# Patch layer of a four-layer network: one scan and one product with C per slot, on 1024 columns instead of 512

## The chip, the cores and the metric

The kernel runs on one core of a Trainium2 chip. The metric is the device time of one launch in microseconds. The kernel's four layers run one after the other in that launch; the change touches only the third, the patch layer (layer 2 in the code).

## The reference

Eight images of 96 channels and 64 x 64 pixels pass through four layers, each a residual: x = x + layer(group_norm(x)). Layer 2, cut to what matters here:

```
xin, z = split(in_proj(x));  z = silu(z)
t = gelu(batch_norm(conv3x3(xin)));  offset = tanh(conv1x1(t)) / 63
x_s = bilinear samples of xin at (pixel grid + offset)
patches: 16 positions each (4 x 4), every patch is a sequence of its own
for 4 directions k (rows, columns, and both reversed):
    delta = softplus(...);  B, C = 16 states each, from x_s
    h[l] = exp(delta[l] * A) * h[l-1] + delta[l] * u[l] * B[l]
    y[l] = sum over states of h[l] * C[l]  + D * u[l]
y = sum of the 4 directions, put back in order
out = out_proj(layer_norm(y) * z)
```

There are 192 inner channels, 16 states and 4 directions. A sequence has only 16 steps: the state starts anew in every patch.

## The kernel before

**Tiling.** An image is cut into 8 chunks of 512 positions, so there are 64 chunks. Within a chunk the recurrence runs over 4 directions x 6 blocks of 32 channels x 2 parts of the states, which makes 48 groups. A group's tile has 128 partitions (32 channels x 4 states) and two halves of 512 columns (two further sets of 4 states). The 32 patches of a chunk lie behind one another along the columns. At each patch's edge the step delta is overwritten with 1e25 (`FAR`, L1493), so the decay there is exp(-huge) = 0 and one long scan restarts at every patch.

**Slots.** The order of the work is written out by hand: `Slots.run` calls `slot(t)` for t in sequence, one slot per group, and what each engine issues in a slot is issued in that order. A chunk takes 48 slots (`PER`) beginning at slot B, and group t is the one scanned in slot t. In slot t:

- SP starts the load of the step sizes `dd` (delta and delta times u, repeated over states by the transfer) for the group six slots ahead (`AHEAD2`). Two groups share one load of 512 KB; four buffers rotate.
- ACT computes the decays `ps_d` of group t+1, exp(A * delta), one instruction per half (L336), into PSUM.
- ACT does the "first" side tasks of the slot: mostly copies of PE's results out of PSUM.
- DVE runs the scan of group t, one instruction per half (L1531), over the decays and in their place in PSUM.
- PE adds the product of group t-1 over the states into `ps_y` with a 0/1 matrix (`total`, L372), and then does its "pe" side tasks.
- ACT does its "act" side tasks.
- POOL computes `dbu` of group t+2, delta u times B, on both halves at once (L354). Then it does its "pool" side tasks.
- DVE multiplies the scanned halves of group t with C into `dbu`, one instruction per half (L364).

Three groups of a chunk's 48 are *late* (groups 2, 26 and 34 of the chunk): their scan writes into `dbu`, and the product with C is done on POOL a slot later (L359) instead of on DVE.

**Side tasks** carry the rest of the layer for this chunk and for the next two: the convolution for the offsets (L1227, copied by L1241, then gelu), the offsets (L1268, copied by L1279, then tanh), the sampling (POOL), the gate (L1396, copied by L1407, then silu), the softplus for delta (L1430 to L1493), the rows of B and C, the layer norm (L1596 to L1625) and the output (L1642 to L1666). Gelu, tanh and silu need another table in ACT than exp and ln, and each is framed by two table loads, the second one bringing back the table for exp.

**The rows of B and C.** `spread` loads, for each direction, 1024 KB of B (`brep`) and 1024 KB of C (`crep`) into SBUF, repeated over the channels. Two buffers of each rotate. The loads are issued by SP at slots T-11 and T-8, T being the direction's first slot; the directions of a chunk run one after the other, 12 slots each.

**Halves of the channels.** Groups of the first 96 channels add into `ps_y0`, those of the last 96 into `ps_y1`. After the first two directions, `rows` copies the sum out in the other pixel order (L1572); after the last two, `columns` adds that copy back with an identity matrix (L1578) and copies the final sum (L1584). `wds` times x (L1542) opens each bank with the D term.

**PSUM.** Eight banks of 512 float32 columns per partition. Decays: `ps_d0` and `ps_d1`, two buffers of one bank each. `ps_y0`, `ps_y1`: one bank each. `ps_k`: one bank for the convolution, the layer norm and the output. `ps_a`: one bank for everything else.

Of the kernel before, what the change touches and what calls it, by code (L numbers as in the profile page):

```python
# [21 lines left out]
NW = 512  # L22
# [224 lines left out]
AHEAD2, SPREAD2 = 6, 4  # L247

# [33 lines left out]
class Slots(Plan):  # L282
# [97 lines left out]
    def steps(self, T, out, f, pre, u, reset):  # L380
# [56 lines left out]
        for n, run in enumerate((add, lost, delta, delta_u)):  # L437
            self.at(T - 15 + 2 * n, "pool", run)

# [696 lines left out]
def layer2(S, src, dst, st_in, st_out, images, cp, W, ready, finish):  # L1136
# [3 lines left out]
    with ExitStack() as ctx:  # L1140
        psd = ctx.enter_context(tc.tile_pool(name="l2q", bufs=2, space=PSUM))
        psy = ctx.enter_context(tc.tile_pool(name="l2y", bufs=1, space=PSUM))
        psk = ctx.enter_context(tc.tile_pool(name="l2k", bufs=1, space=PSUM))
# [11 lines left out]
        sl = Slots(S, cp, wp, psd, "k_red2", GC2, AHEAD2, SPREAD2)  # L1155
# [35 lines left out]
        def front(ch, b, pad, xs, c, B):  # L1191
# [29 lines left out]
            def conv(m, k0, k1):  # L1221
                def run():
                    if k0 == 0:
                        ch["pk"] = new(psk, [128, NW], "ps_k")
                    for k in range(k0, k1):
                        dy, dx = k // 3, k % 3
                        nc.tensor.matmul(  # L1227
                            ch["pk"][:HD, :],
                            woff[:, k, m * HD : (m + 1) * HD],
                            pad[:, dy : dy + 8, dx : dx + IW],  # L1230
                            start=k == 0,
                            stop=k == KT - 1,
                        )

                return run
# [12 lines left out]
            for m, slots, last in (  # L1248
                (0, ((-86, 2), (-85, 2), (-84, 2), (-81, 2), (-80, 1)), -79),
                (1, ((-79, 2), (-67, 2), (-66, 1), (-62, 2), (-61, 2)), -60),  # L1250
            ):
                k = 0
                for t, taps in slots:
                    sl.at(B + t, "pe", conv(m, k, k + taps))
                    k += taps
                sl.at(B + last, "first", conv_out(m))
# [249 lines left out]
        def direction(ch, pr, xs, k, n, T):  # L1506
# [4 lines left out]
            def spread(name, what, t):  # L1511
                def run():
                    dr[name] = new(fp, [128, 4, NW], f"{name}rep", bufs=2)
                    at = n * 2 * NS + what * NS
                    nc.sync.dma_start(
                        dr[name].rearrange("p q l -> p (q l)"),
                        ch["rows"][at : at + NS]
                        .rearrange("(s q) l -> s (q l)", q=4)
                        .unsqueeze(0)
                        .to_broadcast([GC2, HS2, 4 * NW]),  # L1520
                    )

                sl.at(t, "sp", run)

            spread("b", 0, T - 11)
            spread("c", 1, T - 8)

            def scan(i, out, da, dbu):

                way = slice(None, None, -1 if k // 2 else 1)  # L1530
                nc.vector.tensor_tensor_scan(  # L1531
                    out[:, way], da[:, way], dbu[:, way], 0.0, ALU.mult, ALU.add
                )
# [3 lines left out]
            def y_of(h, g, part):  # L1537
                def run():
                    if g == 0 and part == 0 and n % 2 == 0:
                        ch["y", h] = new(psy, [128, NW], f"ps_y{h}")  # L1540
                        if n == 0:
# [4 lines left out]
                    first = n == 2 and g == 0 and part == 0  # L1546
                    return ch["y", h][:HD, :], first, n == 1 and g == HD // GC2 - 1 and part == 1
# [8 lines left out]
            for i in range(12):  # L1556
                part, g, h = i % 2, i // 2 % 3, i // 6
                at = 4 * (i // 2) + 2 * part
                sl.groups[T + i] = Group(
                    n=g, a=acol[:, k, at : at + 2], steps=steps_of(h, g), part=part,  # L1560
                    b=lambda p=part: dr["b"][:, 2 * p : 2 * p + 2, :],
                    c=lambda p=part: dr["c"][:, 2 * p : 2 * p + 2, :],
                    y=y_of(h, g, part), scan=scan, late=12 * n + i in (2, 26, 34),
                )

        def end(ch, im, b, c, B):
# [9 lines left out]
            def columns(h):  # L1576
# [12 lines left out]
                sl.at(B + 42 + 6 * h, "pe", pe)  # L1589
                sl.at(B + 43 + 6 * h, "first", act)  # L1590

            def centred(m):
                def pe():
                    ch["pk"] = new(psk, [128, NW], "ps_k")
# [13 lines left out]
                sl.at(B + 50 + m, "pe", pe)  # L1608
                sl.at(B + 51 + m, "first", act)

            def variance():
                ch["pk"] = new(psk, [128, NW], "ps_k")
# [24 lines left out]
            def out(n):  # L1637
                if n == 0:
                    ch["pk"] = new(psk, [128, NW], "ps_k")
# [30 lines left out]
            sl.at(B + 19, "first", rows(0))  # L1670
            sl.at(B + 25, "first", rows(1))
# [5 lines left out]
            for t, engine, run in (  # L1677
                (53, "pe", variance), (54, "first", root), (55, "dve", scaled),
# [4 lines left out]
            if c == NC - 1:  # L1683
                GroupStats(S, sl, B + 90, st_out[:, b, :], lambda: im["bns"], fp, psk, "ps_k")
# [5 lines left out]
        def piece(n, b, q, m, T0, T):  # L1690
            p, at = {}, slice(q * 1024, q * 1024 + 1024)

            def load():
                p["y"] = new(wp, [128, 1024], "dbu", bufs=6)
                if m < SPREAD2:
                    p["x"] = new(wp, [128, 1024], "dd", bufs=SPREAD2)
                else:
                    x = new(fp, [128, 4, NW], "brep", bufs=2)
# [25 lines left out]
        for n, b in enumerate(images[ready:]):  # L1724
            GroupStats(
                S, sl, 48 * n - 6, st_in[:, b, :], lambda n=n: late_bns[n], fp, psk, "ps_k", nm[b]
            )

        for n, b in enumerate(images):
            im = {"bns": new(fp, [CH, NC, 6], f"bns{n % 2}")}  # L1730
            for c in range(NC):
# [3 lines left out]
                for m, k in enumerate(ORDER):  # L1735
                    T = B + 12 * m
# [449 lines left out]
```

## Time and profile before

| what | value |
|---|---|
| median of 11 runs | 18204.22 us (18178.81 to 18226.62) |
| profiled execution, its own time | 18196.81 us |
| span of its profile | 18195.0 us |
| DVE busy over the span | 16311.3 us (90%) |
| POOL busy | 15215.9 us (84%) |
| PE busy | 13536.2 us (74%) |
| ACT busy | 9807.4 us (54%) |
| mean granted TensorE clock | 0.900 |
| first and last start of the patch layer's scans (L1531) | 3873.7 and 14360.8 us |

The profile is one execution. A row of a group gives line, engine, operation, output and inputs, count, busy time in us and mean ns of one, then the idle time ahead of it and what ended that. The mean of one instruction includes its tail, which overlaps with the next instruction on the same engine; the distance from start to start is shorter. A timeline row gives start, length, engine, line, operation and count; several equal instructions in a row are merged.

### The profile page before, as it was taken

The numbers are of one execution on the slowest core, as the hardware profiler recorded it, in microseconds if no ns is written. First come the engines' busy times: TensorE is split into PE (matmuls) and PEld (weight loads), VectorE is DVE, ScalarE is ACT, GpSimd is POOL, SyncE is SP. The second block draws the span as 40 slices with busy tenths as digits, with TensorE's granted clock in tenths as the row PEclk, the third lists the DMA queues.
The fourth block names the chain that finished last, engine by engine and source line by source line (L and its number), as shares of the span: only waits on it lengthen the run. The fifth ranks groups of instructions, "written<-read, shape, count | busy, mean of one in ns | idle before, by whom it ended". The sixth has DMA issues, their size and how long they took to land. (4 is left out here: it accounts for less than half of the span.)

```text
span 18195.0 us, 132874 instructions
## 1 busy us (share of the span) xinstructions
PE 13536.2 (74%) x32964; PEld 4957.7 (27%) x32964; DVE 16311.3 (90%) x16871; ACT 9807.4 (54%) x16056; POOL 15215.9 (84%) x9068
## 2 busy tenths in 40 slices
PE   8999998968888888888888888888888644434333
PEld 2323223722222222222222222222222211111111
DVE  7999998679999999999999999999999766767667
ACT  6777775556666666666666666666666311111100
POOL 7999996059999999999999999999999656565555
PEclk8999998979999999999999999999999866666666
DMA  7888886366666666666666666666666445444443
GB/s 127 148 150 150 149 149 116 64 157 135 132 134 133 134 134 134 134 134 135 134 134 134 134 134 133 134 135 134 134 133 133 114 134 153 140 143 136 136 128 121
DMA packets 802763, 2437.68 MB, mean 134 GB/s; under 512 B 259122, under 2 KB 260863, under 8 KB 734829
## 3 DMA queue, kind: packets, MB, share of 16 engines
q1 hardware_dynamic: 654541, 1976.06, 54.8%
q0 software_dynamic: 147456, 453.13, 8.2%
q8 instruction: 270, 4.42, 0.1%
q14 instruction: 496, 4.06, 0.1%
HBM read 1116.39 MB, written 104.46 MB: 67 GB/s over the span
## 5 line engine op out<-in xcount | busy, mean ns | idle before, releaser
L354 POOL TENSOR_TENSOR dbu<-dd,brep 128x1024 f32<-128x1024 f32 x3840 | 9020.0, 2364 | 136.0 <-DMA dd<-delta 108.2
L372 PE MATMUL ps_y<-dbu,k_red 128*96 128x512 f32 x15360 | 7506.4, 617 | 1581.4 <-DVE dbu L364 1250.7
L1531 DVE TENSOR_TENSOR_SCAN ps_d<-ps_d,dbu 128x512 f32<-128x512 f32 x5760 | 6713.0, 1209 | 79.6 <-POOL dbu L354 79.4
L336 ACT ACTIVATE ps_d<-dd,l_alog 128x512 f32<-128x512 f32 x7680 | 4989.2, 681 | 3321.9 <-DVE dbu L364 3109.9
L364 DVE TENSOR_TENSOR dbu<-ps_d,crep 128x512 f32<-128x512 f32 x7104 | 4490.9, 672 | 0.0
L372 PEld LDWEIGHTS ps_y<-dbu,k_red 128*96 128x96 f32 x15360 | 2384.6, 167 | 6346.1 <-issue 3707.4
L2020 POOL DMA_INDIRECT v<-t,idx x2304 | 2185.1, 948 | 1573.4 <-DVE s L2047 751.4
L2047 DVE TENSOR_REDUCE s<-v 128x864 f32<-128x3456 f32 x256 | 1554.7, 6073 | 373.7 <-remote 270.9
L2038 DVE TENSOR_TENSOR v<-v,ps_w 128x3456 f32<-128x3456 f32 x256 | 958.3, 3744 | 752.4 <-ACT ps_w L2030 699.6
L681 DVE TENSOR_TENSOR_SCAN ps_d<-ps_d,carry,dbu 128x512 f32<-128x512 f32 x1184 | 1452.9, 1272 | 94.3 <-POOL dbu L354 64.9
L2066 ACT COPY smp<-ps_t 128x768 f32<-128x768 f32 (+1 forms) x512 | 244.3, 529 | 1727.4 <-remote 997.0
L1227 PE MATMUL ps_k<-pad,woff 96*96 96x512 f32 x2304 | 1093.9, 597 | 26.5 <-ACT pad L1204 24.0
L2058 PE MATMUL ps_t<-k_ident,s 128*128 128x128 f32 (+1 forms) x1792 | 323.7, 332 | 955.0 <-issue 683.2
L359 POOL TENSOR_TENSOR dbu<-dbu,crep 128x1024 f32<-128x1024 f32 x288 | 677.8, 2354 | 293.8 <-issue 237.6
L1872 PE MATMUL ps_u<-k_ident,oc 27*128 27x27 f32 x256 | 33.0, 252 | 802.5 <-ACT oc L1867 719.0
L1855 PE MATMUL ps_a<-xpad,l_om 96*27 96x512 f32 x1152 | 592.5, 665 | 20.7 <-issue 20.5
L1227 PEld LDWEIGHTS ps_k<-pad,woff 96*96 96x96 f32 x2304 | 372.3, 164 | 667.5 <-issue 570.2
L2058 PEld LDWEIGHTS ps_t<-k_ident,s 128*128 128x128 f32 (+1 forms) x1792 | 249.6, 169 | 1083.8 <-issue 975.0
L2089 PE MATMUL ps_o<-smp,l_w 128*96 128x512 f32 (+1 forms) x896 | 466.6, 679 | 84.2 <-ACT smp L2066 61.4
L1469 POOL TENSOR_TENSOR sp_m<-sp_m,sp_s 128x512 f32<-128x512 f32 x384 | 489.6, 1275 | 32.2 <-ACT sp_s L1457 32.2
L1176 POOL MEMSET pad<- 96x660 f32 x4 | 2.4, 648 | 610.1 <-DMA y<-yb 610.1
L583 PE MATMUL ps_k<-xn,wk 96*96 96x512 f32 x1024 | 500.6, 612 | 3.1 <-ACT xn L557 2.4
(268 smaller groups left out, 15661.5 us busy)
## 6 DMA issues: line engine op xcount, KB each, us to landing
dd<-delta SPq DMA_DIRECT2D x2304, 512.0 KB
brep<-bcd SPq DMA_DIRECT2D x256, 1024.0 KB
crep<-bcd SPq DMA_DIRECT2D x256, 1024.0 KB
v<-t,idx POOLq DMA_INDIRECT x2304
xo<-x SPq DMA_DIRECT2D x128, 192.0 KB
x<-xo SPq DMA_DIRECT2D x128, 192.0 KB
bcd<-bc SPq DMA_DIRECT2D x64, 256.0 KB
xn<-x SPq DMA_DIRECT2D x64, 192.0 KB
```

What stands on the lines that cost most here:

```text
L336: nc.scalar.activation(da, g.dd[:, 0, :], AF.Exp, scale=g.a[:, i : i + 1])
L354: nc.gpsimd.tensor_tensor(g.dbu, g.dd[:, 1:2, :].to_broadcast([128, 2, NW]), g.b(), ALU.mult)
L359: nc.gpsimd.tensor_tensor(g.dbu, g.dbu, g.c(), ALU.mult)
L364: nc.vector.tensor_tensor(g.dbu[:, i, :], g.h[i], g.c()[:, i, :], ALU.mult)
L372: self.S.nc.tensor.matmul(y, self.red[:, HD - self.gc * (g.n + 1) : 2 * HD - self.gc * (g.n + 1)], g.dbu[:, i, :], start=first and i == 0, ...
L681: nc.vector.tensor_tensor_scan(out, da, dbu, carry[:, n + i : n + i + 1] if c else 0.0, ALU.mult, ALU.add)
L1227: nc.tensor.matmul(ch["pk"][:HD, :], woff[:, k, m * HD : (m + 1) * HD], pad[:, dy : dy + 8, dx : dx + IW], start=k == 0, stop=k == KT - 1,)
L1531: nc.vector.tensor_tensor_scan(out[:, way], da[:, way], dbu[:, way], 0.0, ALU.mult, ALU.add)
L1855: nc.tensor.matmul(im["pa"][: 3 * KT, :], om[:, k, :], xpad[:, 8 * c + dy : 8 * c + dy + 8, dx : dx + IW], start=k == 0, stop=k == KT - 1,)
L2020: nc.gpsimd.indirect_dma_start(out=st["v"][:, k].rearrange("p q c -> p (q c)"), out_offset=None, in_=flat, in_offset=bass.IndirectOffsetOn ...
L2038: nc.vector.tensor_tensor(v3, v3, ps_w[:, g % 2, j * 4 * KT : (j + 1) * 4 * KT] .unsqueeze(2) .to_broadcast([128, 4 * KT, CH]), ALU.mult,)
L2047: nc.vector.tensor_reduce(st["s"], st["v"].rearrange("p k q c -> p k c q"), mybir.AxisListType.X, ALU.add,)
```

## The change

- A new class `WideSlots` replaces `Slots` for this layer. A group's decays are one tile of two banks, three of them rotating (six banks). One scan and one product with C handle 1024 columns. The two exponentials stay two instructions.
- The product of group t is issued in slot t+1, behind the scan of group t+1. The addition over states on PE moves to slot t+2 (late groups t+3). `dbu` has seven buffers instead of six.
- One bank holds y. The groups of a pair of directions are ordered anew: in 24 slots, first all 12 groups of one half of the channels (both directions), then all 12 of the other. So `rows` comes at slots B+14 and B+26, `columns` at B+37 and B+49, each just ahead of the next half's first addition.
- One bank, `ps_a`, holds all the rest. The convolution is laid out over seven slots for each half, and centring and variance move by one slot.
- Each direction has its own buffer of `brep` and `crep` for the pair; loads are issued six slots ahead of the first use.
- Late groups are two per chunk (4 and 28) instead of three.

```diff
+class WideSlots(Slots):
+    def run(self):
+        ts = list(self.plan) + [t + d for t in self.groups for d in (-self.ahead, 3)]
...
+    def slot(self, t):
...
+        g = G(t + 1)
+        if g:
+            g.da = new(self.psd, [128, 2, NW], "ps_d")
+            for i in range(2):
+                nc.scalar.activation(
+                    g.da[:, i, :], g.dd[:, 0, :], AF.Exp, scale=g.a[:, i : i + 1]
+                )
+        self.side(t, "first")
+        g = G(t)
+        if g:
+            g.h = g.dbu if g.late else g.da
+            g.scan(*(v.rearrange("p i l -> p (i l)") for v in (g.h, g.da, g.dbu)))
+        g = G(t - 2)
+        if g and not g.late:
+            self.total(g)
+        self.side(t, "pe")
+        g = G(t - 3)
+        if g and g.late:
+            self.total(g)
+        self.side(t, "act")
+        g = G(t + 2)
+        if g:
+            g.dbu = new(self.pool, [128, 2, NW], "dbu", bufs=7)
+            nc.gpsimd.tensor_tensor(
+                g.dbu, g.dd[:, 1:2, :].to_broadcast([128, 2, NW]), g.b(), ALU.mult
+            )
+        g = G(t - 1)
+        if g:
+            (nc.gpsimd if g.late else nc.vector).tensor_tensor(g.dbu, g.h, g.c(), ALU.mult)
+        for engine in ("pool", "dve", "sp", "end"):
+            self.side(t, engine)
...
-        psd = ctx.enter_context(tc.tile_pool(name="l2q", bufs=2, space=PSUM))
+        psd = ctx.enter_context(tc.tile_pool(name="l2q", bufs=3, space=PSUM))
         psy = ctx.enter_context(tc.tile_pool(name="l2y", bufs=1, space=PSUM))
-        psk = ctx.enter_context(tc.tile_pool(name="l2k", bufs=1, space=PSUM))
         psa = ctx.enter_context(tc.tile_pool(name="l2p", bufs=1, space=PSUM))
...
-                (0, ((-86, 2), (-85, 2), (-84, 2), (-81, 2), (-80, 1)), -79),
-                (1, ((-79, 2), (-67, 2), (-66, 1), (-62, 2), (-61, 2)), -60),
+                (0, ((-81, 1), (-80, 2), (-79, 1), (-78, 1), (-77, 1), (-76, 1), (-75, 2)), -74),
+                (1, ((-67, 1), (-66, 2), (-65, 1), (-64, 1), (-63, 1), (-62, 1), (-61, 2)), -60),
...
-                    dr[name] = new(fp, [128, 4, NW], f"{name}rep", bufs=2)
+                    dr[name] = new(fp, [128, 4, NW], f"{name}rep{(n // 2 + n) % 2}")
...
-            spread("b", 0, T - 11)
-            spread("c", 1, T - 8)
+            spread("b", 0, T - (2 if n % 2 else 8))
+            spread("c", 1, T + (1 if n % 2 else -5))
...
+            for h in range(2):
+                for i in range(6):
+                    part, g, e = i % 2, i // 2, i + 6 * int(h != n % 2)
+                    at = 4 * (3 * h + g) + 2 * part
+                    sl.groups[T + 12 * h + e] = Group(
...
+                        y=y_of(h, e), scan=scan, late=24 * (n // 2) + 12 * h + e in LATE2,
+                    )
...
-                sl.at(B + 42 + 6 * h, "pe", pe)
-                sl.at(B + 43 + 6 * h, "first", act)
+                sl.at(B + 37 + 12 * h, "pe", pe)
+                sl.at(B + 38 + 12 * h, "first", act)
...
-                sl.at(B + 50 + m, "pe", pe)
-                sl.at(B + 51 + m, "first", act)
+                sl.at(B + 51 + m, "pe", pe)
+                sl.at(B + 52 + m, "first", act)
...
-            sl.at(B + 19, "first", rows(0))
-            sl.at(B + 25, "first", rows(1))
+            sl.at(B + 14, "first", rows(0))
+            sl.at(B + 26, "first", rows(1))
...
-                (53, "pe", variance), (54, "first", root), (55, "dve", scaled),
+                (54, "pe", variance), (55, "first", root), (56, "dve", scaled),
...
-                    T = B + 12 * m
+                    T = B + 24 * (m // 2)
```

Wherever the old code took `ps_k` from its own bank, the new code takes `ps_a`.

## The prediction

> **What bounds the kernel now.** I read the busy times by stretch first, to find the stage that the change touches and its fullest engine. The row below is 2000 us from the middle of the patch layer. Its columns are length, then busy time of PE, PEld, DVE, ACT, POOL, then granted clock, DMA share and GB/s.
>
> ```profile
> 8000.00:10000.00 2000.00, 1651.07 (x3654) 569.22 (x3653) 1987.75 (x2297) 1289.01 (x1927) 1956.82 (x1056) 0.99 0.65 134
> ```
>
> DVE is busy 99.4% of the stretch, POOL 97.8%, PE 82.6%, ACT 64%. Next the groups of the same stretch, to price the instructions:
>
> ```profile
> L354 POOL TENSOR_TENSOR dbu<-dd,brep 128x1024 f32<-128x1024 f32 x587 | 1379.6, 2364 | 0.0
> L1531 DVE TENSOR_TENSOR_SCAN ps_d<-ps_d,dbu 128x512 f32<-128x512 f32 x1100 | 1282.0, 1209 | 12.2 <-POOL dbu L354 12.2
> L336 ACT ACTIVATE ps_d<-dd,l_alog 128x512 f32<-128x512 f32 x1172 | 761.0, 681 | 592.6 <-DVE dbu L364 581.0 <-DVE dbu L1531 10.2
> L364 DVE TENSOR_TENSOR dbu<-ps_d,crep 128x512 f32<-128x512 f32 x1099 | 694.6, 672 | 0.0
> L1625 DVE TENSOR_TENSOR yc<-yc,ps_k 96x1024 f32<-96x1024 f32 x13 | 15.7, 1207 | 0.0
> ```
>
> The scan waits for nobody but POOL, and that 12 us in twelve chunks. The exponentials wait for DVE. So DVE sets the pace and POOL is close behind. The waits say where POOL's slack is:
>
> ```profile
> DVE ps_d L1531 <- POOL dbu L354: 12.2, 12, 1.1
> POOL dbu L359 <- issue: 43.2, 12, 3.6
> ```
>
> Once per chunk DVE waits 1.0 us for POOL, and once POOL waits 3.6 us before a late product (it needs the scan). Last, the timelines, because mean durations overlap and only starts give the price of a place in the queue. Two DVE slots, and one late slot (no product on DVE):
>
> ```profile
> 9003.92 2.33 DVE L1531 TENSOR_TENSOR_SCAN ps_d<-ps_d,dbu 128x512 f32<-128x512 f32 x2
> 9006.17 1.26 DVE L364 TENSOR_TENSOR dbu<-ps_d,crep 128x512 f32<-128x512 f32 x2
> 9007.35 2.33 DVE L1531 TENSOR_TENSOR_SCAN ps_d<-ps_d,dbu 128x512 f32<-128x512 f32 x2
> ...
> 9045.07 2.32 DVE L1531 TENSOR_TENSOR_SCAN dbu<-ps_d,dbu 128x512 f32<-128x512 f32 x2
> 9047.32 2.32 DVE L1531 TENSOR_TENSOR_SCAN ps_d<-ps_d,dbu 128x512 f32<-128x512 f32 x2
> ```
>
> A slot is 3.43 us: two scans 2.25, two products 1.18. A late slot is 2.25. The same late scan starts at 8961.76 and 9125.56, so a chunk of 48 slots lasts 163.8 us: 45 x 3.43 + 3 x 2.25 + 1.7 (L1625 and L1663) + 1.0 wait = 163.8. There are 64 chunks. ACT around the gate's table switch, and PE before it:
>
> ```profile
> 9006.87 1.30 ACT L336 ACTIVATE ps_d<-dd,l_alog 128x512 f32<-128x512 f32 x2 [1.61 <-DVE dbu L364]
> 9008.11 0.57 ACT L1407 COPY z<-ps_a 96x512 f32<-96x512 f32 x1
> 9008.70 1.28 ACT L1416 ACT_TABLE_LOAD   x1
> 9010.00 1.06 ACT L1416 ACTIVATE z<-z 96x1024 f32<-96x1024 f32 x1
> 9011.07 1.28 ACT L1417 ACT_TABLE_LOAD   x1
> 9012.37 2.66 ACT L336 ACTIVATE ps_d<-dd,l_alog 128x512 f32<-128x512 f32 x4
> ...
> 9003.56 1.93 PE L372 MATMUL ps_y<-dbu,k_red 128*96 128x512 f32 x4 [0.36 <-POOL dbu L354]
> 9005.32 1.34 PE L1396 MATMUL ps_a<-pad,l_win 96*96 96x256 f32 x4
> ```
>
> From the copy of z to the next exponentials are 4.26 us, longer than a slot. It costs nothing today: the exponentials run up to a slot ahead of the scans.
>
> **DVE's own gain.** 512 columns of a product take 0.535 us more (1207 against 672 ns, L1625 against L364), so two products of 1.18 become one of 1.13. No scan of 1024 is in the trace. At its own rate, 2 x 0.535 us per 512 columns, two scans of 2.25 become one of 2.18; the bounds are 2.25 (nothing saved) and 2.12 (a saving twice the product's). I take 2.18, the same form of instruction with one start fewer. A full slot is 3.31, a late one 2.20. Late groups fall from three to two per chunk, so one more product lands on DVE. Sum: 46 x 3.31 + 2 x 2.20 + 1.7 = 158.4 us.
>
> The Trainium skill (Perfetto Trace Analysis, "Optimizing Scalar/DVE Operations") gives about 125 ns of overhead for each DVE instruction on PSUM. By that figure a slot would save 0.25 us instead of 0.12, and an estimate of DVE's sum would be about 152 us. The starts above show some 60 ns, and I go by them.
>
> **POOL** loses one late product, 2.31 us start to start: 1956.8/2000 x 163.8 - 2.3 = 158.0 us. It hides under any chunk longer than that, and the 1.0 us DVE wait goes as long as DVE is later than POOL anyway. The new row loads (1024 KB) have six slots, about 20 us, instead of nine and eight. SP's queue is passed by the delta loads in the same order, so a late row load would hold those too. No wait for brep or crep is in this stretch now. I put this at zero; if it shows, up to 3 us a chunk.
>
> **What the change adds: ACT loses its lead.** Today decays sit in four banks of one half-group each; exp of t+1 starts when the first product of t-1 ends, half a product before slot t begins, and its second half is needed only 1.13 us into slot t+1. In the changed kernel the product comes a slot later, so the pair for t+1 may start only when slot t has begun (product t-2 ends then), and scan t+1 needs both halves. The whole pair must fall inside slot t. Also its second exponential now waits for the first (one tile): like L1621 behind L1620, which starts 0.68 us after it, so the pair is done after 1.39 and the next ACT step starts after 1.32 (now 1.24). Between two pairs ACT can do 2 x 3.31 - 0.1 - 1.32 - 1.39 = 3.8 us of other work; beyond this DVE stops.
>
> **And one y bank.** Four times a chunk (slots 2, 14, 26, 38) the first matmul of a half must wait for ACT's copy of the previous half, which stands behind an exp pair. PE then runs late, and what is queued behind it on PE is what ACT evicts next. Prices, start to start: a group's matmuls 1.72, a first matmul after a wait 0.1 more, wds 0.86, L1396 1.3, L1596 and L1268 1.72; ACT copies and squares 0.48, L1453/L1460 1.47, L1457 1.37, L1343 0.99. S is a slot's start.
> - Slots 2 to 7: y is copied by S2+2.0; wds, two groups and L1596 end at S4+1.75 instead of before S4. Copy, square, L1457 and L1343 (3.32) hold the pair for 6 until S5+1.76, done 3.15, but slot 5 is late and only 2.20 long: stall 1.0. Slot 5's 2.43 us of evictions and L1460 then make scan 7 late by 0.4.
> - Slots 14 to 17: copy ends S14+2.5, wds, group and gate end S14+6.5 = S15+3.2. Plus 4.26 and 1.39 is S15+8.85; scan 17 is due at 6.62: stall 2.3.
> - Slot 36 (gelu, from L1241's start to the exponentials 4.45): 1.43 + 4.45 + 1.39 = 7.27 against 6.62, with the hand-over 0.7.
> - Slots 38 to 41 (tanh, 4.27): group and L1268 end at S39+2.2, then 2.2 + 4.27 + 1.39 = 7.86: stall 1.3.
> - Slots 25 to 30: the pair for 30 is done 1.7 into slot 29, which lasts 2.20: nothing, with 0.5 to spare.
>
> The other uses of the one ps_a bank (convolution, offsets, output, variance) follow one another without overlap. A convolution slot costs PE 1.72 + 0.86 = 2.58 us of 3.31, with two taps 3.44, and the next slot makes that up: zero, covered by PE's idle time. The last product, a slot later, adds one slot once, 3 us: left out.
>
> Sum 5.7 us. POOL, 6 us below the new chunk, stays hidden. **Chunk: 158.4 + 5.7 = 164.1 us against 163.8**, 64 x 0.3 = 19 us more. Against the profiled run's own 18196.8 us that is 18216; the median of the runs is 7 us above it, so 18223.
>
> The Trainium skill (same page, "Matmuls") says that matmul groups should rotate through PSUM banks so that an eviction overlaps the next group. That speaks against one y bank. By it alone the two-bank layout would keep the turnaround hidden.
>
> **Rivals.**
> *Faster: the y turnaround hides.* If PE is not late, only ACT's lost lead is paid: 1.1 in slots 2 to 7, 0.5 gate, 0.7 gelu, 0.5 tanh, 2.8 in all, chunk 161.2, 166 us less: 18040. For it: PE idles 17% and catches up within a slot. Against: the first group's matmul and the eviction's matmul stand in one queue. With no stall at all it would be 158.8, 17884.
> *Slower: the fourth turnaround counts too.* Slots 25 to 31 hold a y copy, three copies of u, four passes of 1536 columns and a short slot. Once the pair for 30 ends later than 2.2 us into slot 29, the stretch pays like slots 2 to 7, 1.4 us: chunk 165.5, +109 us, 18313; another 0.1 us on each of some fourteen hand-offs brings 18400. For it: every step that I missed adds, none subtracts. Against: 0.5 us of margin.
> *The merge saves nothing on DVE:* slots stay 3.43 and the stalls come on top: 48 x 0.12 = 5.8 us more a chunk, 18590. The 1024-wide product of L1625 speaks against it.
>
> **How the numbers follow.** Forecast 0.45 (18223; alone 18150 to 18290), hidden turnaround 0.24, fourth turnaround 0.27, no merge gain 0.04. The range 18040 to 18400 leaves out the no-stall and no-gain ends. A measurement here tells about 0.2% (36 us, 0.57 us a chunk) from no change. The forecast lies mostly within that, partly above: faster 0.25, same 0.29, slower 0.46.
>
> **What would show it.** Right: DVE's slots 3.31 where ACT is quiet; DVE idle some 5 us a chunk, released by ACT L466 (the new exponentials) and not by POOL, in slots 6, 7, 17, 38, 41; PE waiting for the copies of ps_y; POOL idle about 6 us a chunk. Wrong: DVE still above 99% busy (faster rival), a stall at scans 30 and 31 (slower rival), scans well off 2.2 us, or DVE or POOL waiting for brep or crep.

## The result, and the profile after

The changed kernel takes 18426.89 us (median of 8 runs, 18412.68 to 18447.09) against 18194.83 us of the kernel before on the same chip (31 runs). The ratio is 1.0127, with a 95% interval of 1.0116 to 1.0138. It is slower by 232 us, and lies 27 us above the upper end of the predicted range. The difference lies in the patch layer: from its first scan to its last the traces have 10487.1 us before (3873.7 to 14360.8) and 10712.5 us after (3869.2 to 14581.7), 225 us more.

In the changed kernel's numbering L1584 is the scan, L490 the product, L466 the exponentials, L485 POOL's `dbu`, L373 a group's additions over the states, L1449 and L1460 the gates' matmuls and their copy, L1595 the D term that opens the y bank, L1625 and L1637 the copies of y (`rows` and `columns`), L1649 and L1658 the centring and its copy.

The busy times of the same 2000 us stretch (length, then PE, PEld, DVE, ACT, POOL with their instructions, granted clock, DMA share, GB/s), and below it the groups of that stretch (busy, mean ns, idle before them and its releasers):

```profile
8000.00:10000.00 2000.00, 1659.26 (x3580) 569.49 (x3579) 1906.23 (x1152) 1311.53 (x1898) 1897.49 (x1024) 0.97 0.58 132
...
L485 POOL TENSOR_TENSOR dbu<-dd,brep 128x1024 f32<-128x1024 f32 x576 | 1356.7, 2366 | 74.8 <-PE ps_y L373 66.2 <-DVE ps_d L1584 8.7
L1584 DVE TENSOR_TENSOR_SCAN ps_d<-ps_d,dbu 128x1024 f32<-128x1024 f32 x552 | 1259.4, 2283 | 93.7 <-POOL dbu L485 27.8 <-issue 26.6 <-POOL delta L1536 20.0
L490 DVE TENSOR_TENSOR dbu<-ps_d,crep 128x1024 f32<-128x1024 f32 x551 | 663.5, 1204 | 0.0
```

DVE has fallen from 99.4% to 95.3%, and POOL from 97.8% to 94.9%. No engine is full any more: on DVE 93.7 us stand idle before the scans, in twelve chunks. The granted clock, 0.99 before, is 0.97. The waits of the stretch (total, times, longest):

```profile
ACT z L1460 <- PE ps_a L1449: 36.9, 12, 4.5
PE ps_y L1595 <- ACT yy L1625: 32.2, 12, 2.7
PE ps_y L1595 <- ACT yy L1637: 29.3, 12, 2.4
DVE ps_d L1584 <- POOL dbu L485: 27.8, 6, 5.1
```

PE waits twice a chunk for a y copy, up to 2.7 us, and ScalarE then waits for the gates' matmuls, up to 4.5. The last line needs care: it puts the scan's idle time down to POOL. The ends of the instructions say otherwise. Before each of the stalled scans (6, 7, 17, 38 and 41) in the 50 chunks that are told of below, the scan's own exponentials end 0.1 us ahead of it, 0.5 at most, and POOL's `dbu` for it at least 3.9 us ahead. So it is ScalarE that these scans wait for.

The spacing of the scans gives the chunks. Chunks 8 to 57 of the trace, counted from 0, come in three kinds: about 164.7 us, about 166.4 us and about 170.7 us, with a mean of 167.9 (167.4 over all chunks but the last). The same instructions run in all. PE and ACT from scan 13 on, first in chunk 25 (164.7 us; scan 13 at 8109.17, scan 17 at 8124.78), then in chunk 26 (166.4 us; 8273.90 and 8291.20), here with scan 17 itself. Columns: start, duration, instruction, idle before and its releaser.

```profile
8111.10 1.27 PE L1449 MATMUL ps_a<-pad,l_win 96*96 96x256 f32 x4
8115.06 1.10 PE L1595 MATMUL ps_y<-xs,wds 96*96 96x512 f32 x2 [2.69 <-ACT yy L1625]
8115.99 1.88 PE L373 MATMUL ps_y<-dbu,k_red 128*96 128x512 f32 x4
8117.71 1.27 PE L1449 MATMUL ps_a<-pad,l_win 96*96 96x256 f32 x4
...
8119.02 0.58 ACT L1460 COPY z<-ps_a 96x512 f32<-96x512 f32 x1 [1.68 <-PE ps_a L1449]
8119.62 1.28 ACT L1469 ACT_TABLE_LOAD   x1
8120.91 1.06 ACT L1469 ACTIVATE z<-z 96x1024 f32<-96x1024 f32 x1
8121.98 1.28 ACT L1470 ACT_TABLE_LOAD   x1
8123.28 2.03 ACT L466 ACTIVATE ps_d<-dd,l_alog 128x512 f32<-128x512 f32 x3
```

```profile
8275.83 1.27 PE L1449 MATMUL ps_a<-pad,l_win 96*96 96x256 f32 x4
8279.78 1.20 PE L1595 MATMUL ps_y<-xs,wds 96*96 96x512 f32 x2 [2.69 <-ACT yy L1625]
8280.77 3.52 PE L373 MATMUL ps_y<-dbu,k_red 128*96 128x512 f32 x4
8284.13 1.27 PE L1449 MATMUL ps_a<-pad,l_win 96*96 96x256 f32 x4
...
8285.44 0.58 ACT L1460 COPY z<-ps_a 96x512 f32<-96x512 f32 x1 [3.38 <-PE ps_a L1449]
...
8289.70 2.02 ACT L466 ACTIVATE ps_d<-dd,l_alog 128x512 f32<-128x512 f32 x3
...
8291.20 2.30 DVE L1584 TENSOR_TENSOR_SCAN ps_d<-ps_d,dbu 128x1024 f32<-128x1024 f32 x1 [3.96 <-POOL delta L1536]
```

Up to the y turnaround (the y bank passes from one half of the channels to the other) the two are alike: PE is done with the gates' half 0, then stands 2.69 us for the copy of y. Then one group's four additions take 1.88 us in one chunk and 3.52 us in the other. The gates' half 1 behind them is 1.7 us later, and so are the copy of z, the table pair and scan 17. The windows between scans 14 and 16 (columns as above) name the reason:

```profile
8115.80:8119.10 3.30, 3.30 (x10) 1.48 (x9) 3.30 (x3) 1.47 (x3) 3.30 (x3) 1.00 0.86 130
8280.50:8283.80 3.30, 3.30 (x5) 1.12 (x4) 3.30 (x3) 1.38 (x2) 3.30 (x3) 0.52 0.90 144
```

The granted clock is 1.00 and 0.52. The same thing happens at the end of a chunk's y, in slots 2 to 5: first chunk 25, then chunk 12, one of 170.7 us.

```profile
8073.20 1.10 PE L1595 MATMUL ps_y<-xs,wds 96*96 96x512 f32 x2 [2.44 <-ACT yy L1637]
8074.14 3.60 PE L373 MATMUL ps_y<-dbu,k_red 128*96 128x512 f32 x8
...
8079.49 0.58 ACT L1658 COPY yc<-ps_a 96x512 f32<-96x512 f32 x1 [0.22 <-PE ps_a L1649]
```

```profile
5881.48 2.02 PE L1595 MATMUL ps_y<-xs,wds 96*96 96x512 f32 x2 [2.44 <-ACT yy L1637]
5883.29 5.90 PE L373 MATMUL ps_y<-dbu,k_red 128*96 128x512 f32 x8
...
5890.94 0.58 ACT L1658 COPY yc<-ps_a 96x512 f32<-96x512 f32 x1 [3.39 <-PE ps_a L1649]
```

After the same idle time of 2.44 us eight additions take 3.60 or 5.90 us, and the copy that follows waits 0.22 or 3.39 us. In the 170.7 us kind slot 5 is 6.5 us instead of 3.30 and slot 16 about 8.4 us instead of 5.66.

The trace's record of the granted clock changes only at multiples of 3.413 us. Taking the start of scan 13 modulo 3.413 us, counted from one of these edges, sorts the chunks:

| scan 13 after an edge, us | chunks | length of the chunk, us |
|---|---|---|
| 0.0 to 0.2 | 13 | 166.4 (five of them 166.8 to 168.5) |
| 1.9 to 2.0 | 20 | 169.2 to 171.0, most 170.7 |
| 2.5 to 2.72 | 11 | 164.7, all |
| 2.73 to 3.1 | 6 | 166.2 to 166.6 |

The clock goes with the length in every one of these chunks: slot 16 is 5.7 us in the 11 chunks with slots 14 and 15 at full clock, and 7.2 to 8.5 us in the 39 with a half-clock window there; slot 5 is 3.3 us in the 27 chunks without one in slots 1 to 4, and 4.9 to 6.5 in the other 23. So the phase of a chunk against a clock window that runs by itself decides its length. A chunk of 170.7 us is 50.0 windows long, and so the next one has the same phase: five in succession are of this length (chunks 11 to 15, and again 51 to 55). Per chunk the granted clock is at half for 12.9 us, against 4.9 us in the kernel before.

### The profile page after: what moved, and what is told of

The parts are those of the page before. It is cut to its first block, busy times and chain, and to the rows that moved or that the text cites. A ratio compares the mean times of both kernels' runs of the same rounds, so it can differ in the third digit from the quotient of the medians.

```text
span 18423.5 us, 125611 instructions
## 1 busy us (share of the span) xinstructions
PE 13786.4 (75%) x32964; PEld 5015.1 (27%) x32964; DVE 16075.5 (87%) x10983; ACT 10043.5 (55%) x16056; POOL 15086.7 (82%) x9004
## 4 chain that ended last, share of the span: by engine, by line
DVE 25%; issue 24%; PE 19%; ACT 15%; another core or an unknown queue 9%; POOL 6%; DMA 3%; DVEq 0%; SPq 0%; POOLq 0%; ACTq 0%
DVE ps_d L1584 15%; PE ps_y L373 7%; ACT ps_d L466 5%; DVE dbu L490 5%; DMA dd<-delta 2%; POOL dbu L485 2%; PE ps_k L637 2%; PE ps_a L1908 2%; POOL delta L1530 1%; DVE ps_d L735 1%; DVE v L2091 1%; DVE s L2100 1%; PE ps_o L2142 1%; PE ps_y L1595 1%
## 5 line engine op out<-in xcount | busy, mean ns | idle before, releaser
L373 PE MATMUL ps_y<-dbu,k_red 128*96 128x512 f32 x15360 | 7707.4, 629 | 1368.1 <-DVE dbu L490 1128.3
L485 POOL TENSOR_TENSOR dbu<-dd,brep 128x1024 f32<-128x1024 f32 x3072 | 7232.9, 2365 | 444.6 <-PE ps_y L373 392.8
L1584 DVE TENSOR_TENSOR_SCAN ps_d<-ps_d,dbu 128x1024 f32<-128x1024 f32 x2944 | 6717.5, 2284 | 542.9 <-POOL dbu L485 208.8
L466 ACT ACTIVATE ps_d<-dd,l_alog 128x512 f32<-128x512 f32 x6144 | 4229.9, 690 | 3379.3 <-DVE dbu L490 3270.0
L373 PEld LDWEIGHTS ps_y<-dbu,k_red 128*96 128x96 f32 x15360 | 2429.7, 169 | 6271.9 <-issue 3072.6
L490 DVE TENSOR_TENSOR dbu<-ps_d,crep 128x1024 f32<-128x1024 f32 x2944 | 3546.0, 1205 | 0.0
L1280 PE MATMUL ps_a<-pad,woff 96*96 96x512 f32 x2304 | 1129.5, 595 | 25.6 <-ACT pad L1257 24.0
L337 ACT ACTIVATE ps_d<-dd,l_alog 128x512 f32<-128x512 f32 x1536 | 999.5, 682 | 166.6 <-DMA dd<-delta 113.8
L365 DVE TENSOR_TENSOR dbu<-ps_d,crep 128x512 f32<-128x512 f32 x1344 | 850.7, 674 | 0.0
L1280 PEld LDWEIGHTS ps_a<-pad,woff 96*96 96x96 f32 x2304 | 378.1, 164 | 646.0 <-issue 593.9
L1483 PE MATMUL ps_a<-xs,wd 97*128 97x512 f32 x768 | 429.4, 641 | 135.0 <-ACT sp_m L1496 129.6
```

The lines of the kernel that those rows point to most:

```text
L337: nc.scalar.activation(da, g.dd[:, 0, :], AF.Exp, scale=g.a[:, i : i + 1])
L373: self.S.nc.tensor.matmul(y, self.red[:, HD - self.gc * (g.n + 1) : 2 * HD - self.gc * (g.n + 1)], g.dbu[:, i, :], start=first and i == 0, ...
L466: nc.scalar.activation(g.da[:, i, :], g.dd[:, 0, :], AF.Exp, scale=g.a[:, i : i + 1])
L485: nc.gpsimd.tensor_tensor(g.dbu, g.dd[:, 1:2, :].to_broadcast([128, 2, NW]), g.b(), ALU.mult)
L490: (nc.gpsimd if g.late else nc.vector).tensor_tensor(g.dbu, g.h, g.c(), ALU.mult)
L1280: nc.tensor.matmul(ch["pk"][:HD, :], woff[:, k, m * HD : (m + 1) * HD], pad[:, dy : dy + 8, dx : dx + IW], start=k == 0, stop=k == KT - 1,)
```

## The experiments

They ran on three chips. The kernel before takes 17352.67 us on the one of runs 1 to 4 (median of 9 runs), 18197.04 on the one of runs 5 to 8 (9 runs) and 17354.27 on the one of runs 9 to 11 (7 runs). Ratios are to the kernel before on the same chip. The chips differ outside the patch layer: from the span less the time from its first scan to its last, the rest of the launch takes 6867 to 6872 us in runs 1, 3, 9 and 11 and 7736 us in run 8. Chunks are the spacing of the scans in the profiled run (chunks 8 to 57); the kind of 164.7 us shows on the chips of runs 3 and 8 alike.

**1. The copies of y a slot earlier.**

```
-                sl.at(B + 38 + 12 * h, "first", act)
+                sl.at(B + 37 + 12 * h, "act", act)
...
-            sl.at(B + 14, "first", rows(0))
-            sl.at(B + 26, "first", rows(1))
+            sl.at(B + 13, "act", rows(0))
+            sl.at(B + 25, "act", rows(1))
```

> The four copies of y (rows, columns) are issued at the end of the slot before instead of behind the next slot's exponentials. Theory (PE is late after the y turnaround, and its idle gap of 2.7 us puts it on half rate; both delay ACT's evictions): PE starts the next half without the gap, no matmul of the gate or of the centring runs at half rate, the stall before scan 17 falls from 2.3 to 4.1 us to about 0.5, the one before scan 6 to about 0.7, the one before scan 41 to about 0.5. Chunk 161 to 162 us instead of 167.4: about 18050 us, faster than before by 0.8%. Rival (ACT's lost lead alone, the turnaround hides): nothing moves, 18430. Rival (POOL takes over as soon as DVE is quicker): chunk not below 163, 18150.

17236.63 us (17233.35 to 17237.96), ratio 0.9932 (0.9919 to 0.9946): 0.7% faster than the kernel before, with a move of the four copies of y. All chunks are 161.9 to 162.3 us, as the theory expected. PE's waits for y in the same stretch, 29.3 us in twelve chunks for L1637 before the move, shrink:

```profile
PE ps_y L1595 <- ACT yy L1637: 8.0, 12, 0.7
```

With idle times that short the half clock falls to 3.9 us per chunk, none of it in slots 2 or 14. The stalls that are left come to 3.2 us: 0.8 before scan 6, 0.5 before 7, 0.6 before 17, 0.8 before 38 and 0.6 before 41.

**2. The same with late group 9 for 4.**

```
-LATE2 = (4, 28)
+LATE2 = (9, 28)
```

> As e1, and the late groups are 9 and 28 instead of 4 and 28, so slot 5 is a full slot of 3.31 us. Theory: the stall before scan 6 comes only from slot 5 being 2.20 us long where ACT has most to do; it goes, and scan 7 keeps 0.3: 1 us a chunk less than e1, about 17985. Rival (POOL): its late product now stands in slot 10 among the delta steps, scans 11 to 19 wait for POOL, same as e1 or above it.

17225.57 us (17224.84 to 17230.71), ratio 0.9927 (0.9914 to 0.9941), mean chunk 161.9. The stall before scan 6 went as expected, but slot 16 grew from 3.91 to 4.74 in the mean (4.55 in 21 of 50 chunks, 5.24 in 18). A stall moved, and next to nothing was gained. Two causes are possible, and this run doesn't part them: the short slot, now slot 10, brings scan 17's due time 1.1 us forward against the gates; and the half clock is back, 8.8 us per chunk against 3.9 in run 1, most of it in slots 10 to 12, just ahead of the gates.

**3. More matmuls in the gaps, as a test of the clock.** Half 0 of the gates twice, the first u product three times, and two unused products behind the second columns.

```
+                    for _ in range(3 if j == 0 else 1):
...
-                    for k in range(2):
+                    for k in (0, 1, 0, 1) if m == 0 else (0, 1):
...
+                if h:
+                    sl.at(B + 49, "pe", warm)
```

> The y copies stay where they are; some matmuls of slots 13, 25 and 1 are repeated (the gate's first half once, the first u product twice, two unused products behind the second columns), so PE idles 1 to 1.6 us before a y turnaround instead of 2.7. Nothing of the result changes. Theory (the half rate after the gap makes the difference between 164.7 and 167.4 us a chunk): every chunk takes 164.7, scan 17 waits 2.3 us in all of them, 18255. Rival (the spread between chunks has another cause, POOL or a transfer): still 167.4, 18430.

17467.16 us (17462.94 to 17470.62), ratio 1.0066 (1.0051 to 1.0082). More work on PE halves the loss. The result lies between theory and rival: the 170.7 us kind is gone and the half clock is down to 7.6 us per chunk, but 27 of 50 chunks are still of the 166.4 us kind. Where the clock drops in slot 15, the window before it held 1.84 us of PE work.

**4. The product back in its scan's own slot**, additions and y copies one slot earlier with it.

```
             g.scan(*(v.rearrange("p i l -> p (i l)") for v in (g.h, g.da, g.dbu)))
+            if not g.late:
+                nc.vector.tensor_tensor(g.dbu, g.h, g.c(), ALU.mult)
-        g = G(t - 2)
+        g = G(t - 1)
         if g and not g.late:
             self.total(g)
```

> The product goes back into the scan's own slot, the additions and the y copies one slot earlier; everything else stays. Theory (the product a slot later takes ACT's lead away): ACT may run a slot ahead again, the stalls at the table switches (scans 17, 38, 41) and at scans 6 and 7 vanish, and each product waits for its scan's end instead, 2.28 + 0.03 + 1.13 = 3.44 us a slot: chunk 46 x 3.44 + 2 x 2.20 + 1.7 = 164.3, 18225. Rival (the lead does not matter, y turnaround and clock do it): slots of 3.44 and the stalls on top, chunk 170 or more, 18600.

17916.73 us (17913.18 to 17923.9), ratio 1.0324 (1.031 to 1.034), chunk 172.9 where 164.3 was expected. That is the rival's size (170 or more), but not by the stalls that it named. Two readings. The stalls before scans 6, 7, 17 and 38 vanish: with the decay bank free a slot earlier ScalarE has its lead, as the prediction said. But a slot is 3.53 us (3.44 expected) and not 3.32, as the product now waits for the scan in front of it and starts 2.39 us after it instead of 2.20. And the one y bank costs more here: slot 40 is 7.2 us and slot 39 4.1 in the mean, because PE stands 3.8 us in slot 37 for the columns' copy behind gelu and then goes on at half clock.

**5. No table changes:** gelu, silu and tanh are left out, with a plain copy in place of each.

```
-                nc.scalar.activation(ch["z"], ch["z"], AF.Silu)
-                nc.scalar.preload_act_table_set(LOG_EXP)
+                nc.scalar.activation(ch["z"], ch["z"], AF.Identity)
```

and the same for gelu and tanh.

> The gelu, silu and tanh of the patch layer are replaced by plain copies and their table reloads left out, so those functions are not computed. Theory (ScalarE's lead of about one slot is used up by three things: a table pair, the wait for the y bank, and TensorE at half clock behind that wait): the stalls before scans 38 and 41 (0.8 and 1.3 us) vanish and the one before scan 17 falls from 2.3 to 5.2 us to at most 1 us, as the gates' copy may come late without a silu and a reload behind it; the stalls before scans 6 and 7 stay (1.1 and 0.5 us), and in some chunks a 6.5 us slot 5. Chunk 160.5 to 162 us, ratio to the kernel before about 0.985. Rival (the tables set nothing; the half clock alone does): the stall before scan 17 stays at 3 us or more in half of the chunks, chunk 165 to 166 us.

18127.89 us (18096.18 to 18135.25), ratio 0.9953 (0.9938 to 0.9969; about 0.985 was expected), chunks mostly of 161.5 and 163.1 us, mean 162.8: between the two theories. The stalls before scans 38 and 41 vanish and slot 16 is 4.2 us in the mean instead of 7.4. Slot 5 is 3.3 us in 15 of 50 chunks, as at full clock in the changed kernel, and 5.0 in the 35 with a half-clock window in slots 1 to 4: these 1.7 us are the half clock's, with no table pair near them. In 18 chunks a new stall of 1.0 us stands before scan 30, again behind a half-clock window. So the tables turn a late gate into a stall, but are not the cause of all.

**6. Half 0 of the gates four times, the first u product four times**, otherwise as run 3.

> As the run with repeated matmuls, with more of them: half 0 of the gates is multiplied four times (about 1.3 us more TensorE work in the gap behind it), the first u product four times. The output is the same. Theory (the clock is halved after a 3.41 us window in which TensorE was busy for less than about half of it; the gap behind the gates' half 0 makes such a window): no half-rate window is left in slots 14 to 16, the slot before scan 17 is 5.7 us in every chunk, all chunks are 164.5 to 165 us against 166.4 and 170.7 of the changed kernel. Rival (what is late is the y turnaround itself, not the clock): the slot before scan 17 stays at 7.2 us in half of the chunks or gets longer, as the added work stands before the additions, chunk 165.5 us or more.

18414.43 us (18378.47 to 18424.44), ratio 1.0118 (1.0103 to 1.0134). Chunk and slot 16 are what the rival expected, the clock is what the theory expected, and both have their reason. The granted clock of a middle stretch is full,

```profile
6000.00:8000.00 2000.00, 1689.63 (x3831) 598.01 (x3831) 1903.89 (x1149) 1313.21 (x1895) 1892.60 (x1022) 1.00 0.58 131
```

and the kinds are gone: 48 of 50 chunks are 167.2 to 167.6 us. But they are long, since each pass of the gates takes 1.1 us, not the 0.43 that I had put. Four of them ended 6.5 us after scan 13 instead of 3.2, and the copies behind them started at 6.56 instead of 4.78. Slot 16 is 7.45 us: the 5.66 of full clock and these 1.8. Slot 29 is 2.92 instead of 2.20 in most chunks, the stall that the fourth-turnaround rival spoke of; together with the 1.8 that makes 167.2 out of 164.7.

**7. What the runs pointed to, moved together:** the copies of run 1, late groups 20 and 28, silu one slot later, gelu and the offsets one later, tanh two later, the chunk's output one later.

```
-LATE2 = (4, 28)
+LATE2 = (20, 28)
...
-            sl.at(B - 60, "act", gelu)
+            sl.at(B - 59, "act", gelu)
...
-            sl.at(B - 57, "act", tanh)
+            sl.at(B - 55, "act", tanh)
...
-            sl.at(T + 2, "act", silu)
+            sl.at(T + 3, "act", silu)
```

> The version that the experiments point to: the y copies in the slot before (as in the run with early copies), late groups 20 and 28 in place of 4 and 28, silu one slot later, gelu one slot later and tanh two slots later with what hangs on them. Theory: no stall of over 0.5 us is left but one beside a table pair; slots 41 x 3.32 + 2 x 2.2 + the slots of the scaling and the statistics; chunk 159.5 to 161 us against 162.0 of the run with early copies and 163.8 of the kernel before; ratio to the kernel before 0.980 to 0.988. Rival (each table pair costs its time wherever it stands, as ScalarE has no spare time in a chunk): chunk 161.5 to 162.5 us, ratio 0.992 to 0.995.

18018.29 us (18001.26 to 18063.11), ratio 0.991 (0.9893 to 0.9926), chunk 161.4, between theory and rival. The stalls of slots 5 and 16 are gone and tanh costs 0.3 instead of 0.6, but the slot beside gelu grew from 4.10 to 5.44 us.

**8. The changed kernel again.**

> The changed kernel again, unaltered, beside the other runs on this chip. Theory and rival alike: ratio to the kernel before 1.012 to 1.016, chunks of 164.7, 166.4 and 170.7 us with a mean of about 167.4 us; if the kinds are mixed in another proportion, the mean goes with it, and the half-rate time per chunk (12 to 13 us) with the mean.

18437.03 us (18420.21 to 18447.1), ratio 1.0128 (1.0113 to 1.0144). Mean chunk 167.5, half clock 12.1 us per chunk, and the phases sort the kinds in the same way: of the twelve with scan 13 at 2.56 to 2.70 us after an edge all but one are 164.7 or 165.1, and all fifteen at 1.91 to 2.07 are 170.6 to 171.0.

**9. Filler that fits:** two and a half passes of the gates' half 0, otherwise as run 3.

```
-                    for k in (0, 1, 0, 1) if m == 0 else (0, 1):
+                    for k in (0, 1, 0, 1, 0) if m == 0 else (0, 1):
```

> As the run with the gates' half 0 four times, with two and a half passes of it in all: they end at 4.9 us after scan 13 starts, where ScalarE gets to their copy at 4.8, so that the copies start 0.1 us later at most (four passes ended at 6.5 and put everything behind them 1.8 us later). The first u product three times, two unused products behind the second columns; the output is the same. Theory (a 3.41 us window with TensorE busy for less than about 1.9 us halves the clock of the next one): no half-rate window in slots 14 and 15, the slot before scan 17 is 5.7 to 5.9 us in every chunk, all chunks are 164.7 to 165.0 us, ratio to the kernel before 1.002 to 1.006. Rival (the kinds of chunk come from something else that goes with the phase): the 166.4 us kind stays in a third of the chunks or more, mean 165.5 us or more.

17459.4 us (17439.51 to 17465.11), ratio 1.0061 (1.0044 to 1.0078), mean chunk 165.3. 38 of 50 chunks are 164.8 to 165.2 us with slot 16 at 5.8; the other twelve are 166.5 or 166.6. PE around the turnaround in one of the 38:

```profile
8045.93 2.94 PE L1450 MATMUL ps_a<-pad,l_win 96*96 96x256 f32 x10
8050.02 1.10 PE L1596 MATMUL ps_y<-xs,wds 96*96 96x512 f32 x2 [1.16 <-ACT yy L1626]
8050.96 1.88 PE L373 MATMUL ps_y<-dbu,k_red 128*96 128x512 f32 x4
```

The wait for y ends only 0.1 us later than it did (6.0 us after scan 13 starts, 5.9 in chunk 25 of the changed kernel), but PE stood 1.16 us and not 2.69 before it, and the additions run at full clock. Of the longer kind 27 chunks have become 12, all twelve with scan 13 in the first 0.9 us after an edge. In no other phase does it occur. That is the theory's mechanism, and the size was over-promised. The theory's limit of 1.9 us doesn't hold by the recorded times either: in these twelve chunks the window before the drop held 2.26 to 2.32 us of PE work, so that some 1.1 us of idle time in it was enough.

**10. The merge with the old number of banks:** as run 4, with four banks for decays, two for y and two for the rest.

```
-        psd = ctx.enter_context(tc.tile_pool(name="l2q", bufs=3, space=PSUM))
+        psd = ctx.enter_context(tc.tile_pool(name="l2q", bufs=2, space=PSUM))
```

and two buffers each in the pools of ps_y and ps_a.

> The one scan and one product of 1024 columns alone, with the banks as before: four for decays, two for y, two for the rest, and the product in its scan's own slot. Theory: no y turnaround is left, so no stall at scans 6, 30 or 41 and no late gates from it; but the product waits for its scan (3.53 us a slot in place of 3.32) and the exps of the scan after next wait until the product has freed both banks of a pair, so ScalarE's lead is at most 1.2 us and each slot with more than that of other ScalarE work stalls: 45 slots of 3.53, two late ones of 2.3, the scaling and the statistics, and 4 to 10 us of stalls, chunk 169 to 176 us. Rival (the merge is sound and the single y bank is what loses the time): chunk below 164 us.

17746.94 us (17735.83 to 17754.77), ratio 1.0227 (1.021 to 1.0244), chunk 170.3, as the theory expected (169 to 176). Slot 40 is down from 7.2 to 3.71 us, and no wait of PE for a copy of y is left in the stretch, so a second y bank does end the turnaround. The stalls that are left come to 1.5 us a chunk, where 4 to 10 were expected. The product's wait remains in each slot:

```profile
7999.83 1.23 DVE L475 TENSOR_TENSOR dbu<-ps_d,crep 128x1024 f32<-128x1024 f32 x1
8001.15 2.30 DVE L1586 TENSOR_TENSOR_SCAN ps_d<-ps_d,dbu 128x1024 f32<-128x1024 f32 x1
8003.55 1.23 DVE L475 TENSOR_TENSOR dbu<-ps_d,crep 128x1024 f32<-128x1024 f32 x1
```

The scan starts at 8001.15, ends at 8003.45, and its product starts at 8003.55. From scan to scan it is 3.53 us, against 3.43 of the kernel before with its halves. In these runs the merge pays only with the product a slot later, as the changed kernel has it with its third pair of banks; a later product with two pairs was not tried.

**11. As run 7 with gelu and the offsets left where they were.**

> As the moved version, with gelu and the offsets back in their old slots (there the slot beside gelu went from 4.10 to 5.44 us by the move) and tanh two slots later. Theory: slot 37 is 4.10 us again, the rest as in the moved version, chunk 161.4 less 1.3 = 160.1 us, ratio to the kernel before 0.981 to 0.986. Rival (with gelu earlier and tanh later the stall moves on to tanh's slot): chunk 161 to 161.8 us, ratio 0.988 to 0.992.

17110.71 us (17103.03 to 17114.47), ratio 0.9859 (0.9842 to 0.9875): faster than both kernels. The chunk is 160.0 us in 41 of 50, as worked out. DVE is busy 99.5% of the stretch again:

```profile
6000.00:8000.00 2000.00, 1710.58 (x3750) 581.35 (x3751) 1989.08 (x1202) 1369.41 (x1980) 1974.05 (x1066) 0.99 0.60 137
```

## Why the prediction was wrong

The side of the result was the likeliest one, at 0.46; the size was missed by 204 us. Luck has a part in the side: the forecast lay 19 us above the kernel before, less than the 36 us that it said could be told from no change, and what makes the result clearly slower is the term that it lacked. By the prediction's own steps:

**DVE's own gain: right.** Ordinary slots are 3.317 us (3.31 forecast), late ones 2.197 (2.20). The rival that the merge saves nothing has fallen. Its working gives 1.125 + 1.07 = 2.195 us for the wide scan, not the 2.18 that it took, and 2.197 was measured; over 46 slots this is the 0.3 us by which DVE's sum comes out higher. In the same way its rival without any stall stands at 158.8 us, where its own sum is 158.4. Some 57 ns per instruction are what the slot shows. The estimate from the 125 ns that the Trainium skill ("Perfetto Trace Analysis", "Optimizing Scalar/DVE Operations") gives for DVE on PSUM would have made a slot 3.18.

**POOL: right.** It is busy 94.9% of a 167.4 us chunk, 158.9 us (158.0 forecast), and no stall comes from it, by the ends of `dbu` given above. Its idle time is 8.5 us a chunk, where about 6 were forecast, as the chunk is longer. No wait for brep or crep is among the waits of the stretch.

**ACT's lead and the turnaround, at full clock: right.** In chunks of the 164.7 us kind the stalls are:

| before scan | forecast, us | measured, us |
|---|---|---|
| 6 | 1.0 | 1.1 |
| 7 | 0.4 | 0.5 |
| 17 | 2.3 | 2.3 |
| 38 | 0.7 | 0.8 |
| 41 | 1.3 | 1.3 |

None is at scan 30, so the rival of the fourth turnaround fell too. The sum is 6.0 against 5.7, and the chunk 164.7 against 164.1. That ScalarE's lead is behind them is what run 4 speaks for, where they vanish with the lead restored, all but the one at scan 41, which the turnaround makes longer. A slot is also 0.2 us longer there, which gives ScalarE more time; but run 10, with the same slots and only two pairs of banks, has stalls of 0.2 to 0.6 us at the same scans again. The share of the turnaround is shown by run 1: with the copies earlier the stall before scan 17 falls from 2.3 to 0.6 us and the one before scan 41 from 1.3 to 0.6.

**The step that failed: PE's prices behind a wait.** The working took each group's matmuls at 1.72 us and "a first matmul after a wait 0.1 more". They are prices at full clock. The change leaves PE idle for 2.4 to 2.7 us, twice a chunk, just ahead of a dense stretch of matmuls, and in 39 of 50 chunks the granted clock is then halved for a window or two: four additions cost 3.5 us instead of 1.9, right on the chain to the gates and to the centring. The terms that were mis-sized are slots 14 to 17 (stall before scan 17: 2.3 forecast, 3.9 in the mean of all chunks, as slot 16 is 7.22 and not 3.32) and slots 2 to 6 (before scan 6: 1.0 forecast, 2.2 in the mean). Over the full-clock chunk that is 1.6 (7.22 less 5.66) and 1.1 us (slot 5, 4.39 less 3.29). The sum: 1.6 + 1.1 + the 0.6 by which the full-clock chunk itself is above the forecast = 3.3 us a chunk, times 64 = 211 us, against the 204 missed. Runs 6 and 9 show the cause by taking the half clock away: in run 6, at full clock, 48 of 50 chunks have one length within 0.4 us, and in run 9 the chunks of 170.7 us are gone and the long ones are down to the twelve that still have a drop. The kernel before has half-clock windows too, 4.9 us of them per chunk, and yet nearly all its chunks are 163.8 to 164.2 us: there ScalarE's lead may well cover a late matmul, which no run here tests. So its trace held rows at half clock to price with, and the 0.99 of its stretch row hid them. One of them, of the kernel before, in which eight additions after an idle time of 3.20 us take 5.37 us:

```profile
8154.01 5.37 PE L372 MATMUL ps_y<-dbu,k_red 128*96 128x512 f32 x8 [3.20 <-POOL dbu L359]
```

The page that bears on this is the Trainium skill's "TensorE: Matmul & The Clock Gate": in "Part 1: The HAM clock gate" it says that a free-running window of 3413 ns decides between half and full rate, and the table under "Why this matters for your kernels" advises against PE idle for more than about 3 us between bursts. The window's length and the two rates agree with the clock record here. The limit does not: 2.44 and 2.69 us were enough. What goes with a drop is the work in the window before it. In the changed kernel's patch layer the window before a drop held 1.28 us of PE work in the median of 172 drops, and at most 1.8 us; of 2736 windows at full clock that no drop followed, 99 in 100 held over 1.7 us, the least 1.4. So little work goes with a drop, but there is no sharp limit by the recorded times: run 9 has drops after windows with 2.3 us of repeated matmuls of 256 columns. What exactly is counted stays open.

**What would show it: one item misread.** DVE's idle time is there, in the slots named, but it isn't put down to ACT L466 in the main; the groups name POOL and issue. The ends tell more: before each stalled scan the exponentials are the last of the two to end, as said above.

The faster rival's price, 161.2 us for a hidden turnaround, was good: run 1, which hides most of it, has 162.0. Left open: why gelu one slot later lengthens its stall by 1.3 us (run 7 against run 11).

## What to carry to other kernels

A price from a trace holds at the clock it was measured at: before adding a wait to TensorE, add up how much work is left in a 3.4 us window around it, and if it is about half or less (here the drops followed windows with up to 1.8 us, in run 9 up to 2.3), price the next 3.4 to 7 us of matmuls at twice their time as well. When one kernel's repeated unit shows several lengths with the same instructions, sort them by their phase against that window before looking for another cause. And the order on an engine's queue can be worth more than the instructions saved: here a merge that saves 0.11 us a slot lost 1.3%, and the same merge with copies, late groups and two table pairs placed elsewhere gained 1.4%.

## What was not expected of the hardware

- A chunk length that is a whole number of clock windows repeats itself: at 170.67 us, 50.0 windows of 3.413 us, chunks stay at one phase for five in succession, at the slowest of the three kinds.
- Extra matmuls made the program faster: half-clock time per chunk fell from 12 to 13 us to 4.8 (run 9), and the ratio to the kernel before from 1.0127 to 1.0061.
- An instruction of DVE that needs the result of the one just before it on the same engine starts 0.10 us after that one's end. An independent one starts before the recorded end (2.20 us after the start of a 2.28 us scan). Per slot of one scan and one product the dependent order costs 0.2 us (3.53 against 3.32).
